# Gathering some source columns on VectorE and ScalarE: earlier address loads, 24 columns each, one-hot rows six groups ahead

## The chip, the cores and the metric

The kernel runs on one core of a Trainium2 chip. The metric is the device time of one execution in microseconds (us). Engines are named as in the profile: PE is TensorE's matrix multiplication, PEld its weight load, DVE is VectorE, ACT is ScalarE, POOL is GpSimd, SP is SyncE. PEq, DVEq and ACTq are the sequencers of those engines, which read the program in order, execute register instructions themselves and hand the others to the engine.

## The reference

One layer of a graph network on 12500 nodes with 64 features and 212500 edges with 32 features; the edges are sorted by their destination. All is float32.

```
msg_in     = concat(nodes[src], nodes[dst], edge_features)      # 212500 x 160
messages   = relu(msg_in @ mW1 + mb1) @ mW2 + mb2               # 128 hidden, 64 out
aggregated = segment_sum(messages, dst)                         # 12500 x 64
out        = layernorm(x + relu(concat(x, aggregated) @ uW1 + ub1) @ uW2 + ub2)
```

## The kernel before, in words

**Groups.** The edges are cut into G = 554 groups of 384 edges, three tiles of 128 (the last group has two). For a group the kernel needs the rows `x[src]` of its 384 edges, turned so that features lie along partitions. There are two ways to get them:

- By gather: one indirect DMA on POOL for each tile (line 165 of the profile is that call in `gather`) brings 128 rows of 64 features into `own_s`, and TensorE transposes the tile (L369) into PSUM; ScalarE copies the result into `own_st` (L380).
- By column copies: the whole transposed node table lies on the chip in `own_xc`, one column of 64 features for each node. For the first tile of some groups (the list `COPIED`, the "columned" groups) no gather is issued. Instead 128 small instructions copy one column each, from an address held in a register, straight into `own_st`: a COPY on VectorE (L539) or an ACTIVATE on ScalarE (L541). The copied groups' first tile is still transposed, but only its one-hot part is taken.

In each step COLS = 44 columns are copied, in four blocks: 12 and 8 on VectorE (`VCOLS`), 12 and 12 on ScalarE (`ACOLS`). So 128 columns, one tile, are ready every 128/44 = 2.9 steps, and 180 of the 1661 tiles need no gather; 1481 gathers are left. The addresses of a block's columns are read from a small table (`index`) into registers of the engine's own sequencer by one TENSOR_LOAD (function `registers`, L520; `fetch` then issues the copies). The copies start with step BEGIN = 18 and end ten steps before the last (`SHORT`).

**One step.** Step k, for most of the loop, gives TensorE one unbroken run of matrix multiplications over three groups: the transposes of group k (L369), the hidden layer of group k-2 (L395), and the sums of group k-4 by destination (L423, and the edge counts, L428). One signal at the end of the run releases what follows: ScalarE's copy (L380), VectorE's ReLU (L406), and VectorE's two additions of the sums into `own_agg` and of the counts into a row of `own_xc` (L437, L438). The results lie in two sets of PSUM buffers that alternate, so the run of step k starts after the ReLU, the copy and the additions of step k-2.

**The one-hot rows** (L357): VectorE compares each edge's destination with the 32 nodes of the group's window and writes three 128x32 patterns beside the gathered rows. The transposes of group k wait for them; they are written two groups ahead, in step k-2, between VectorE's two blocks of columns.

**Order.** The program's order on each engine is that in which the code issues it. In a step before the change, VectorE's order is: ReLU, TENSOR_LOAD of 12 addresses (queued in `between` and issued inside `add`, ahead of the first addition), two additions, 12 copies, one-hot rows of group k+2, TENSOR_LOAD of 8 addresses, 8 copies. ScalarE's is: copy L380 (two, for a columned group), TENSOR_LOAD of 12, 12 copies, TENSOR_LOAD of 12, 12 copies. Once in four steps VectorE's sequencer also loads the four start nodes of the next groups (`places`, L319), and once in eight VectorE turns a fresh table of node numbers into addresses (L505).

**POOL** gathers in program order, group k+16 being issued in step k. A ring of 20 buffers (`RING`) holds the gathered rows, so a gather waits at most for the transposes of the group 20 before. SP moves edge features, window rows and address tables.

**Updates.** Whenever a chunk of 512 nodes has all its edges (25 chunks, one about every 23 steps), six small stages of the node update are spread over six steps (`step_update`), each behind TensorE's run of the step: matrix products (L448 to L450, L462, L463), ReLU and square root on ScalarE (L456, L478), statistics and scaling on VectorE (L471, L472, L483, L486).

## Time and profile before

| what | value |
|---|---|
| time, median of 3 runs (lowest to highest) | 1880.31 us (1878.53 to 1881.24) |
| the profiled execution's own time | 1876.62 us |
| its span, first to last instruction | 1874.9 us |
| mean granted TensorE clock | 0.967 |
| busy share of the span: PE, DVE, ACT, POOL | 76%, 80%, 83%, 75% |
| memory traffic over the span | 53 GB/s |

The span is what the trace covers; the execution's own time is 1.7 us more. A row of the timeline gives start, duration, engine, line, operation, tiles and count, and in brackets how long the engine had sat idle before it and who ended that. A row of the waits gives the total, the number of times and the longest. A row that groups a line's instructions gives the busy time, the mean of one, and the idle time before them. TENSOR_LOAD is a sequencer's instruction and not counted as busy; it is seen when a line's instructions are asked for, with its shortest, median and longest duration.

### The profile page before, as it was taken

Reading aid. Unit: us, or ns where it says so; the run is one execution under the profiler, and the core shown is the slowest. Engines: PE = TensorE matmul, PEld = TensorE weight load, DVE = VectorE, ACT = ScalarE, POOL = GpSimd, SP = SyncE. Lnnn points to the kernel's source line nnn. Section 1 sums busy time; section 2 is a strip of 40 time slices with the busy share of each in tenths; the row PEclk is TensorE's granted clock in tenths of the full one; section 3 lists DMA queues with packets and bytes.
Section 4 is the critical chain, followed back from the end, with each engine's and each line's share of the span. In section 5 each row is a group of like instructions: output and inputs, shape, how many; then the busy total and the mean of one; then the engine's idle time right before and its main releaser. Section 6 shows DMA issues by size and latency. Waiting matters only on the chain. (4 is left out here: it accounts for less than half of the span.)

```text
span 1874.9 us, 61070 instructions
## 1 busy us (share of the span) xinstructions
PE 1429.1 (76%) x12373; PEld 1252.6 (67%) x12373; DVE 1491.0 (80%) x13140; ACT 1552.1 (83%) x13372; POOL 1399.1 (75%) x1488
## 2 busy tenths in 40 slices
PE   3898878778777778687776786776877777867777
PEld 3886667677676677576665676665656666666665
DVE  2458888888888888887887878878888788787873
ACT  3268998988998988988988889889888888898971
POOL 7777777777777777777777777777777777777773
PEclk9999999999999999999999989999999999999998
DMA  4442222222122212211221212212121212121220
GB/s 126 134 117 61 51 53 49 51 53 52 47 54 53 51 48 54 50 49 47 52 54 46 53 47 52 52 46 54 49 49 50 51 49 53 45 55 48 51 50 22
DMA packets 94294, 104.48 MB, mean 56 GB/s; under 512 B 39230, under 2 KB 61366, under 8 KB 93910
## 3 DMA queue, kind: packets, MB, share of 16 engines
q0 software_dynamic: 47392, 48.60, 11.7%
q1 hardware_dynamic: 45888, 51.46, 9.6%
q14 instruction: 280, 2.29, 0.4%
q8 instruction: 104, 1.70, 0.4%
q10 hardware_dynamic: 630, 0.43, 0.1%
HBM read 90.61 MB, written 9.62 MB: 53 GB/s over the span
## 5 line engine op out<-in xcount | busy, mean ns | idle before, releaser
L165 POOL DMA_INDIRECT own_s<-in_x,src_sb x1481 | 1398.4, 944 | 452.5 <-issue 303.3
L541 ACT ACTIVATE own_st<-own_xc 64x4 uint8 x12560 | 1268.1, 192 | 64.3 <-issue 56.0
L539 DVE COPY own_st<-own_xc 64x4 uint8 x10480 | 893.8, 190 | 20.8 <-issue 1.1
L369 PE MATMUL own_ps<-own_ident,own_s 128*96 128x128 f32 x1661 | 292.3, 287 | 396.8 <-issue 116.7
L395 PE MATMUL own_ps<-own_wm,own_st 128*128 128x128 f32 x3322 | 482.7, 284 | 0.0
L423 PE MATMUL own_ps<-own_s,own_h 128*128 128x128 f32 x3322 | 480.0, 282 | 2.6 <-DVE own_h L406 2.0
L369 PEld LDWEIGHTS own_ps<-own_ident,own_s 128*96 128x96 f32 x1661 | 171.1, 134 | 463.4 <-issue 234.9
L380 ACT ACTIVATE own_st<-own_ps 96x384 f32<-96x384 f32 (+2 forms) x734 | 294.0, 401 | 190.2 <-PE own_ps L428 149.3
L423 PEld LDWEIGHTS own_ps<-own_s,own_h 128*128 128x128 f32 x3322 | 433.4, 199 | 5.0 <-DVE own_h L406 3.8
L395 PEld LDWEIGHTS own_ps<-own_wm,own_st 128*128 128x128 f32 x3322 | 434.4, 199 | 1.8 <-issue 0.8
L406 DVE TENSOR_SCALAR own_h<-own_ps 128x384 f32<-128x384 f32 x553 | 302.0, 546 | 141.4 <-PE own_ps L428 97.3
L437 DVE TENSOR_TENSOR own_agg<-own_ps,own_agg 128x32 f32 x554 | 106.0, 191 | 147.2 <-DVE own_h L406 95.1
L428 PE MATMUL own_ps<-own_s,own_one 128*1 128x32 f32 x3322 | 188.8, 194 | 0.0
L428 PEld LDWEIGHTS own_ps<-own_s,own_one 128*1 128x1 f32 x3322 | 113.6, 83 | 69.1 <-issue 4.9
L438 DVE TENSOR_TENSOR own_xc<-own_ps,own_xc 1x32 f32 x554 | 102.0, 184 | 48.4 <-PE u_ps L450 31.7
L357 DVE TENSOR_TENSOR own_s<-iota,dlc 128x96 f32<-128x96 f32 x554 | 137.4, 248 | 0.7
L331 PE MATMUL u_ps<-w1b,own_xc 65*128 65x128 f32 x196 | 52.0, 416 | 30.9 <-DMA own_wm<-in_mW 16.3
L331 PEld LDWEIGHTS u_ps<-w1b,own_xc 65*128 65x128 f32 x196 | 47.2, 324 | 33.2 <-DMA own_wm<-in_mW 16.2
L462 PE MATMUL u_ps<-u,u 128*128 128x64 f32 (+1 forms) x196 | 63.1, 405 | 0.5 <-ACT u L456 0.5
L463 PE MATMUL u_ps<-same,own_xc 65*128 65x64 f32 (+1 forms) x196 | 62.3, 403 | 0.0
L462 PEld LDWEIGHTS u_ps<-u,u 128*128 128x128 f32 (+1 forms) x196 | 54.2, 325 | 2.4 <-ACT u L456 0.8
L463 PEld LDWEIGHTS u_ps<-same,own_xc 65*128 65x128 f32 (+1 forms) x196 | 54.9, 328 | 0.0
(60 smaller groups left out, 268.2 us busy)
## 6 DMA issues: line engine op xcount, KB each, us to landing
own_st<-in_efT SPq DMA_DIRECT2D x138, 192.0 KB
own_s<-in_x,src_sb POOLq DMA_INDIRECT x1481
own_wm<-by_dst SPq DMA_DIRECT2D x554, 16.0 KB
by_dst<-t SPq DMA_DIRECT2D x24, 256.0 KB
out<-o SPq DMA_DIRECT2D x24, 128.0 KB
own_xc<-in_xT SPq DMA_DIRECT2D x12, 179.2 KB
index<-in_src_copied SPq DMA_DIRECT2D x65, 1.4 KB
dlc_i<-in_dst_cols SPq DMA_DIRECT2D x1, 831.0 KB
```

Source lines behind the costliest of these rows:

```text
L165: nc.gpsimd.indirect_dma_start(out=s[:p, j, :D], out_offset=None, in_=x[:, :], in_offset=bass.IndirectOffsetOnAxis(ap=src_sb[:p, g * TG + ...
L357: places_by[g] = nc.vector.tensor_tensor(own.s[g % RING][:, :, D:], iota.unsqueeze(1).to_broadcast([P, TG, W]), dlc[:, g * TG : (g + 1) * ...
L369: nc.tensor.transpose(xt[:, j * P : j * P + p], s[:p, j, :], ident[:p, :p])
L380: after(nc.scalar.activation(t[r, c : c + n][:, m], xt[r, m], AF.Copy), step))
L395: nc.tensor.matmul(pre[:p, j, :], t[:, c + j * P : c + j * P + p], wm[g % NW], start=True, stop=True)
L406: relu_by[g] = [nc.vector.tensor_scalar(h, pre, 0.0, None, ALU.max)]
L423: did.append(nc.tensor.matmul(sg, h[:p, j, :], s[:p, j, D:].unsqueeze(1).to_broadcast([p, TIMES, W]), start=j == 0, stop=j == len(sizes) - 1))
L428: did.append(nc.tensor.matmul(counted, own.one[:p], s[:p, j, D:], start=j == 0, stop=j == len(sizes) - 1))
L462: nc.tensor.matmul(y[:p, k], u[:, k:q:n], u2, start=True, stop=False)
L463: nc.tensor.matmul(y[:p, k], xc[: D + 1, base + k : base + q : n], same, start=False, stop=True)
L539: by[engine] = nc.vector.tensor_copy(o, x_at)
L541: by[engine] = nc.scalar.activation(o, x_at, AF.Copy)
```

## The change

Four things are done. VectorE copies 12 and 12 columns in a step, not 12 and 8, so that COLS is 48; with that the list `COPIED` has 196 groups, and 1465 gathers are left. The first TENSOR_LOAD of VectorE and that of ScalarE are issued ahead of the step, that is ahead of the ReLU and of copy L380, and no longer behind them. The two additions follow the ReLU with nothing between. The one-hot rows are written six groups ahead (`LEAD`), not two.

VectorE's order in a step is then: TENSOR_LOAD of 12, ReLU, two additions, 12 copies, one-hot rows of group k+6, TENSOR_LOAD of 12, 12 copies. ScalarE's is: TENSOR_LOAD of 12, copy L380, 12 copies, TENSOR_LOAD of 12, 12 copies.

```diff
+LEAD = 6
-VCOLS = (12, 8)
+VCOLS = (12, 12)
 ...
             count = xc[COUNT : COUNT + 1, at]
-            if between:
-                between.pop()()
             a = after(nc.vector.tensor_tensor(agg[:, at], sg[:, 0, :], agg[:, at], ALU.add), step)
 ...
-    onehot(0)
-    onehot(1)
+    for g in range(LEAD):
+        onehot(g)
 ...
         if k < G - SHORT:
-            between.append(lambda: registers(k, 0))
+            registers(k, 0)
+            registers(k, len(VCOLS))
             step((turn, k), *([(hidden, k - 2)] if k > 1 else []),
                  *([(sums, k - 4)] if k > 3 else []))
             made, summed = max(0, k - 1), max(0, k - 3)
-            if between:
-                between.pop()()
-            fetch(0)
+            fetch(0, len(VCOLS))
 ...
         window(k + SB)
-        onehot(k + 2)
+        onehot(k + LEAD)
         if k < G - SHORT:
             for part in range(1, len(VCOLS + ACOLS)):
-                registers(k, part)
-                fetch(part)
+                if part != len(VCOLS):
+                    registers(k, part)
+                    fetch(part)
```

More of the change, by code (lines that the diff above doesn't have):

```diff
@@ L588, in ordered @@
     made = summed = 0
-    between, held = [], {}
+    held = {}
     for k in range(G):
```

## The prediction, made before the change was run

> **What bounds the kernel now.** The page comes first: its first line, the busy shares, the costliest group.

> ```profile
> span 1874.9 us, 61070 instructions
> PE 1429.1 (76%) x12373; PEld 1252.6 (67%) x12373; DVE 1491.0 (80%) x13140; ACT 1552.1 (83%) x13372; POOL 1399.1 (75%) x1488
> L165 POOL DMA_INDIRECT own_s<-in_x,src_sb x1481 | 1398.4, 944 | 452.5 <-issue 303.3
> ```

> No engine looks full, and POOL looks idlest of the four. That misleads: a gather takes 944 ns and has (452.5 / 1481 =) 306 ns of idle time ahead of it. The waits tell what that idle time is.

> ```profile
> POOL own_s L165 <- issue: 303.3, 995, 0.3
> ...
> POOL own_s L165 <- DMA own_s<-in_x,src_sb: 116.1, 381, 0.3
> ...
> DVE own_agg L437 <- DVE own_h L406: 95.1, 232, 0.9
> ...
> ACT own_st L541 <- issue: 56.0, 176, 0.7
> ```

> Whatever is named as the releaser, POOL's longest gap is 0.3 us, as long as the mean one. So POOL waits for nothing; 0.3 us is what lies between any two gathers, and POOL is full from end to end: (1398.4 + 452.5) / 1481 = 1.25 us a gather, 1851 of 1875 us. A step has 3 - 44/128 = 2.656 gathers, 3.32 us. **POOL sets the pace.** With 48 columns a step has 2.625 gathers, 3.28 us.

> Can the others follow that? Around 400 us, where POOL is still groups ahead, the timeline shows them at their own pace. VectorE:

> ```profile
> 402.43 0.54 DVE L406 TENSOR_SCALAR own_h<-own_ps 128x384 f32<-128x384 f32 x1
> 402.97 0.19 DVE L437 TENSOR_TENSOR own_agg<-own_ps,own_agg 128x32 f32 x1
> 403.19 0.18 DVE L438 TENSOR_TENSOR own_xc<-own_ps,own_xc 1x32 f32 x1
> 403.41 0.94 DVE L539 COPY own_st<-own_xc 64x4 uint8 x12
> 404.27 0.24 DVE L357 TENSOR_TENSOR own_s<-iota,dlc 128x96 f32<-128x96 f32 x1
> ...
> 405.00 0.54 DVE L406 TENSOR_SCALAR own_h<-own_ps 128x384 f32<-128x384 f32 x1
> 406.02 0.19 DVE L437 TENSOR_TENSOR own_agg<-own_ps,own_agg 128x32 f32 x1 [0.48 <-DVE own_h L406]
> 406.24 0.18 DVE L438 TENSOR_TENSOR own_xc<-own_ps,own_xc 1x32 f32 x1
> 406.46 0.97 DVE L539 COPY own_st<-own_xc 64x4 uint8 x12
> ...
> 408.08 0.54 DVE L406 TENSOR_SCALAR own_h<-own_ps 128x384 f32<-128x384 f32 x1
> ...
> 410.74 0.54 DVE L406 TENSOR_SCALAR own_h<-own_ps 128x384 f32<-128x384 f32 x1
> ```

> Copies start 0.072 us apart (403.41 to 404.27 holds twelve). From ReLU to ReLU it is 2.57, 3.08, 2.66 us. What holds VectorE up is not on the page at all: the TENSOR_LOADs of its sequencer. Asked for by line, in short stretches (the third row, of ScalarE, for comparison):

> ```profile
> L520 DVEq TENSOR_LOAD <-index x1: 593/593/593, 403.6 to 403.6; - x1
> L520 DVEq TENSOR_LOAD <-index x1: 846/846/846, 405.0 to 405.0; - x1
> L520 ACTq TENSOR_LOAD <-index x4: 772/778/786, 402.9 to 407.1; - x4
> L520 DVEq TENSOR_LOAD <-index x2: 593/720/848, 406.7 to 407.6; - x2
> L319 DVEq TENSOR_LOAD <-start_i x139: 339/344/626, 12.3 to 1841.7; - x139
> ```

> Eight addresses take 0.59 us, twelve 0.85, and meanwhile the sequencer hands its engine nothing; the engine lives on what it was handed before. Three things are read from these rows:

> - *How far the sequencer gets ahead.* The load of eight starts 0.2 us behind the first copy of a block (403.6 for 403.41, 406.7 for 406.46). The third copy is then running, and nine copies and the one-hot rows have been handed on: ten instructions, no more.
> - *How fast it hands on.* From the load of eight (406.7, ends 0.59 later) to the load of twelve (407.6) it hands on eight copies and the ReLU, in 0.3 to 0.4 us, taken as 0.37: 0.04 each, less than the 0.072 that a copy runs.
> - *What a load costs that nothing covers.* The load of 405.0 stood behind the ReLU of 405.00 and ended at 405.85; the addition came at 406.02. Of that 0.17, 0.08 is the addition's own address arithmetic; an instruction follows a load by 0.09.

> A walk along VectorE's sequencer, load of eight to load of eight, gives 0.59 + 0.37 + 0.85 + 0.17 + 0.22 + 0.22 + 0.20 = 2.62 us; the timeline has 2.66. With the start nodes' load in a step, 0.34 more, it has 3.08. The walk holds, and VectorE today has over half a microsecond to spare in POOL's 3.32.

> **The change, part by part.**

> *16 gathers fewer.* 16 x 1.25 = 20 us, if POOL still sets the pace.

> *ScalarE.* It keeps its 24 columns.

> ```profile
> 402.39 0.47 ACT L380 ACTIVATE own_st<-own_ps 96x384 f32<-96x384 f32 x1
> 402.76 2.39 ACT L541 ACTIVATE own_st<-own_xc 64x4 uint8 x24
> 405.16 0.66 ACT L380 ACTIVATE own_st<-own_ps 32x128 f32<-32x128 f32 x2
> ```

> From copy to copy 2.77 us, columns without a break. Its loads are 0.78 against 12 x 0.1 us of columns; the moved load lies beneath the last ten columns (0.95 us) of the step before. ScalarE stays near 2.8 us and gains at most the 56 us of the last waits row above, off the path.

> *VectorE, the second block: 8 to 12.* The load is 0.85 for 0.59, and four more instructions are handed on at 0.04: 0.26 + 0.16 = 0.42 us more along the walk.

> *VectorE, the first load ahead of the ReLU.* Before, this load was handled while VectorE ran the last copies and the ReLU (0.54), and only its end showed. Now the ReLU itself stands behind it, and with the ReLU the additions. What can run beneath it is the rest of the second block: twelve copies are 0.86 us of work, but they start only 0.09 behind the second load and 0.48 of them pass while they are being handed on, so about 0.45 is left against 0.85 + 0.09. **VectorE stands idle for about 0.5 us in each step** unless it would be waiting for TensorE anyway. The new walk, second load to second load:

> second load 0.85; twelve copies handed on 0.48; first load 0.85; ReLU starts 0.09; ReLU to addition 0.54 (402.43 to 402.97); addition to addition 0.22; to the first copy 0.22; to the next second load 0.20. Sum **3.45 us**. The start nodes' load (0.34 and 0.04 to hand it on, one step in four) adds 0.10: **3.55 us**, against POOL's 3.28.

> No row shows this order, so I bound it. If no load ever showed, a step is the engine's work: 0.54 + 0.44 + 24 x 0.072 + 0.24 = 2.95 us. If nothing covered them, 2.95 + 1.70 = 4.65 us. I take 3.45 because the same walk gives the present order to 0.04 us.

> [...]

> *Is TensorE ready?* If its run ended late, the first load would lie beneath that wait. It doesn't: TensorE's run that released the ReLU of 408.08 ended with

> ```profile
> 406.38 0.34 PE L428 MATMUL own_ps<-own_s,own_one 128*1 128x32 f32 x6
> ```

> at 406.72, 1.36 us earlier, and the next run needs only the additions of two steps before. With VectorE slower it waits longer. POOL, ahead at 3.28, is stopped by its ring of 20, which costs nothing.

> *The additions right behind the ReLU* end the 95 us of the waits, all from ReLU to addition; they come back as the idle time ahead of the ReLU, counted above. *One-hot rows six ahead* are the same instructions earlier; a run that waits for additions does not notice. Four more ahead of the loop are 4 x 0.24, 1 us at most. SP's transfers stay as they are.

> *Updates.* VectorE's part adds to a step that it bounds:

> ```profile
> L486 DVE TENSOR_SCALAR o<-u_ps,mv,rstd 128x64 f32<-128x64 f32 x96 | 26.4, 337 | 1.0
> ...
> L471 DVE BATCH_NORM_STATS2 stats<-u_ps 128x6 f32<-128x64 f32 x96 | 19.9, 207 | 1.1 <-PE u_ps L463 0.6
> L472 DVE BATCH_NORM_AGGREGATE mv<-stats 128x2 f32<-128x6 f32 x96 | 17.5, 182 | 3.3
> ```

> (26.4 + 19.9 + 17.5) / 24 = 2.66 us an update, 23 of them inside the loop: 61 us.

> *The sum*, with the transposes counted in three stretches:

> ```profile
> 0.00:138.00 138.00, 14.76 (x78) 12.64 (x78) 0.98 0.46 127
> 138.00:1811.00 1673.00, 270.83 (x1545) 154.10 (x1545) 0.97 0.21 51
> 1811.00:1875.00 64.00, 6.73 (x38) 4.35 (x38) 0.89 0.12 29
> ```

> Three transposes are a step: 26 steps of start, bound by first loads and left at 138 us; 515 steps with columns; a tail without columns, left at 64 us (a few less, as no gather is awaited there). 138 + 515 x 3.55 + 61 + 64 = 2091 us of span. The profiled execution took 1876.62 us, 1.7 more than its span, so 2093; the median of the runs lies 3.7 us above that execution: **2097 us, 11% slower**.

> **The rivals.**

> *POOL stays the pace (faster).* Then 16 gathers go: 1876.6 - 20 + 3.7 = 1860 us. For it: the moved loads are free wherever the engine waits for TensorE, and the two last waits rows show 95 and 56 us of such standing. It decides if a plain step of VectorE is at most 3.28 - 0.10 - 0.12 (update, 61 / 515) = 3.06 us, that is if 0.4 us more of the first load were covered. Against it: let a run of TensorE end on POOL's beat. VectorE starts its second load 1.18 us later, ends it at 2.03, has handed on the block at 2.51, ends the first load at 3.36, and the ReLU comes at 3.45, late for 3.28 with nothing else in the step. 0.11.

> *Half of the idle time is covered* (the sequencer starts its second load sooner than the rows show, or copies lie longer beneath the first): 3.30 us by 515 is 129 us less, 1968 us, counted from 1960 to 2030. 0.10.

> *A shorter queue than ten.* [...] 0.04.

> *The change does nothing of the kind* (VectorE's extra work and the 16 gathers cancel): 1880 us. 0.02.

> **How the numbers follow.** The forecast, 2097, has 0.70, with a range of its own of 2030 to 2150 (a step of 3.43 to 3.65). Something slower still without a place of its own has 0.03. 1960 to 2150 takes in forecast and half cover, 0.80. Measurement of this kernel can tell 0.2%, 4 us, from no change: faster 0.11, same 0.02, slower 0.87.

> **What would show it.** Right: from ReLU to ReLU 3.4 to 3.6 us all through the run; a gap of some 0.5 us ahead of each ReLU, with a TENSOR_LOAD of 0.85 in it; ReLU to addition always 0.54; TensorE and ScalarE waiting for VectorE; gaps of POOL well over 0.3 us. Wrong: POOL's gaps still 0.3 us at 1465 gathers, or ReLUs 3.3 us apart that start as TensorE's run ends. The sum fails if the second load starts earlier than 1.2 us behind the ReLU, or if an update costs other than 2.7 us.

## The result, and the profile after

The changed kernel takes 2073.39 us (median of 4 runs, 2069.49 to 2075.81), the kernel before beside it 1880.46: a ratio of 1.103, 95% interval 1.102 to 1.105. The forecast was 2097, the range 1960 to 2150. The profiled execution took 2073.34 us, its span 2071.5.

The page of the changed kernel, whose lines answer to the first ones shown of before (L166 is the gather, L370 the transposes, L381 ScalarE's copy, L407 the ReLU):

```profile
span 2071.5 us, 63093 instructions
PE 1459.8 (70%) x12373; PEld 1278.8 (62%) x12373; DVE 1667.8 (81%) x15212; ACT 1531.0 (74%) x13364; POOL 1384.9 (67%) x1472
...
L166 POOL DMA_INDIRECT own_s<-in_x,src_sb x1465 | 1384.1, 945 | 601.5 <-issue 394.9
...
L407 DVE TENSOR_SCALAR own_h<-own_ps 128x384 f32<-128x384 f32 x553 | 307.6, 556 | 289.8 <-PE own_ps L429 153.5
```

The 16 gathers are gone, and a gather takes what it took (945 ns). But the idle time ahead of the gathers has risen from 452.5 to 601.5 us: POOL waits now. The idle time ahead of the ReLU has doubled, from 141.4 us in the trace of before to 289.8. VectorE's share of busy time, 81% for 80%, shows nothing of this, although VectorE is now what everything waits for. The waits of the changed kernel:

```profile
POOL own_s L166 <- issue: 394.9, 1265, 5.2
...
PE own_ps L370 <- ACT own_st L381: 368.1, 268, 2.8
ACT own_st L381 <- PE own_ps L429: 328.0, 318, 9.8
POOL own_s L166 <- PE own_ps L429: 194.5, 164, 5.9
```

POOL's longest gap was 0.3 us and is 5.9: it is stopped by its ring. ScalarE's copies wait for TensorE (328 us). And TensorE, by the name in the second row, waits for ScalarE's copy. That name is wrong, and the timeline of the three engines shows how one finds out. VectorE, two steps, the first cut short, and the beginning of a third:

```profile
1213.39 0.56 DVE L407 TENSOR_SCALAR own_h<-own_ps 128x384 f32<-128x384 f32 x1 [0.29 <-PE own_ps L429]
1213.87 0.18 DVE L436 TENSOR_TENSOR own_agg<-own_ps,own_agg 128x32 f32 x1
1214.08 0.18 DVE L437 TENSOR_TENSOR own_xc<-own_ps,own_xc 1x32 f32 x1
...
1217.63 0.56 DVE L407 TENSOR_SCALAR own_h<-own_ps 128x384 f32<-128x384 f32 x1 [0.68 <-issue]
1218.10 0.18 DVE L436 TENSOR_TENSOR own_agg<-own_ps,own_agg 128x32 f32 x1
1218.32 0.18 DVE L437 TENSOR_TENSOR own_xc<-own_ps,own_xc 1x32 f32 x1
1218.53 1.01 DVE L538 COPY own_st<-own_xc 64x4 uint8 x12
1219.46 0.24 DVE L358 TENSOR_TENSOR own_s<-iota,dlc 128x96 f32<-128x96 f32 x1
1219.67 0.99 DVE L538 COPY own_st<-own_xc 64x4 uint8 x12
1220.97 0.56 DVE L407 TENSOR_SCALAR own_h<-own_ps 128x384 f32<-128x384 f32 x1 [0.32 <-issue]
```

ScalarE's copy and TensorE's runs at the same place:

```profile
1213.17 0.47 ACT L381 ACTIVATE own_st<-own_ps 96x384 f32<-96x384 f32 x1
```

```profile
1212.72 0.34 PE L429 MATMUL own_ps<-own_s,own_one 128*1 128x32 f32 x6
1214.37 0.50 PE L370 MATMUL own_ps<-own_ident,own_s 128*96 128x128 f32 x3 [1.31 <-ACT own_st L381]
...
1216.14 0.34 PE L429 MATMUL own_ps<-own_s,own_one 128*1 128x32 f32 x6
```

The copy ends at 1213.64; the run starts 0.73 us later. VectorE's second addition ends at 1214.08 + 0.18 = 1214.26, and the run starts 0.11 us behind that. Over the steps between 300 and 1800 us, three quarters of TensorE's runs start 0.10 us behind that addition; in the trace of before the least was 1.21. A run starts after the additions of two steps before, so the run of 1214.37, released by the addition of 1214.08, belongs to the third ReLU shown, that of 1220.97. It ended at 1216.48, 4.5 us before that ReLU; the run before it, which belongs to the ReLU of 1217.63, ended at 1213.06, 4.57 us before. So these ReLUs don't wait for TensorE, and the name in the bracket of the first one (its own run had ended at 1210.13) is wrong too. From 1217.63 to 1220.97 it is 3.34 us, and of the 0.32 us of idle time ahead of the ReLU of 1220.97 the sequencer's loads are the cause:

```profile
L519 DVEq TENSOR_LOAD <-index x2: 846/850/853, 1218.7 to 1220.0; - x2
```

Two loads of 0.85 us, 1.3 us from start to start; the second ends at 1220.89, and the ReLU of 1220.97 comes 0.09 us behind it.

### The profile page after: what moved, and what is told of

It is laid out like the page before. It is cut to its first block, busy times and chain, and to the rows that moved or that the text cites. A ratio compares the mean times of both kernels' runs of the same rounds, so it can differ in the third digit from the quotient of the medians.

```text
span 2071.5 us, 63093 instructions
## 1 busy us (share of the span) xinstructions
PE 1459.8 (70%) x12373; PEld 1278.8 (62%) x12373; DVE 1667.8 (81%) x15212; ACT 1531.0 (74%) x13364; POOL 1384.9 (67%) x1472
## 4 chain that ended last, share of the span: by engine, by line
PE 48%; ACT 23%; issue 13%; DVE 9%; DMA 3%; ACTq 3%; DVEq 1%; SPq 0%
PE own_ps L424 13%; PE own_ps L396 13%; ACT own_st L540 13%; ACT own_st L381 10%; PE own_ps L370 9%; DVE own_st L538 6%; PE own_ps L429 5%; ACTq L519 3%; PE u_ps L461 2%; PE u_ps L462 2%; PE u_ps L332 1%; DMA by_dst<-t 1%; PE u_ps L447 1%; PE u_ps L449 1%; PE u_ps L448 1%
## 5 line engine op out<-in xcount | busy, mean ns | idle before, releaser
L166 POOL DMA_INDIRECT own_s<-in_x,src_sb x1465 | 1384.1, 945 | 601.5 <-issue 394.9
L540 ACT ACTIVATE own_st<-own_xc 64x4 uint8 x12536 | 1245.6, 192 | 0.5
L538 DVE COPY own_st<-own_xc 64x4 uint8 x12552 | 1031.3, 184 | 35.3 <-issue 7.9
L370 PE MATMUL own_ps<-own_ident,own_s 128*96 128x128 f32 x1661 | 298.2, 291 | 537.0 <-ACT own_st L381 368.1
L381 ACT ACTIVATE own_st<-own_ps 96x384 f32<-96x384 f32 (+2 forms) x750 | 299.8, 400 | 438.4 <-PE own_ps L429 328.0
L370 PEld LDWEIGHTS own_ps<-own_ident,own_s 128*96 128x96 f32 x1661 | 173.1, 135 | 603.6 <-ACT own_st L381 387.0
L407 DVE TENSOR_SCALAR own_h<-own_ps 128x384 f32<-128x384 f32 x553 | 307.6, 556 | 289.8 <-PE own_ps L429 153.5
L424 PE MATMUL own_ps<-own_s,own_h 128*128 128x128 f32 x3322 | 493.2, 288 | 2.6 <-DVE own_h L407 2.0
L396 PE MATMUL own_ps<-own_wm,own_st 128*128 128x128 f32 x3322 | 492.5, 287 | 0.0
L424 PEld LDWEIGHTS own_ps<-own_s,own_h 128*128 128x128 f32 x3322 | 446.5, 204 | 5.0 <-DVE own_h L407 3.8
L396 PEld LDWEIGHTS own_ps<-own_wm,own_st 128*128 128x128 f32 x3322 | 444.2, 203 | 2.0 <-issue 0.8
L437 DVE TENSOR_TENSOR own_xc<-own_ps,own_xc 1x32 f32 x554 | 101.9, 184 | 20.2 <-PE u_ps L449 2.9
L436 DVE TENSOR_TENSOR own_agg<-own_ps,own_agg 128x32 f32 x554 | 100.7, 182 | 12.3 <-PE own_ps L429 10.2
```

Source lines behind the costliest of these rows:

```text
L166: nc.gpsimd.indirect_dma_start(out=s[:p, j, :D], out_offset=None, in_=x[:, :], in_offset=bass.IndirectOffsetOnAxis(ap=src_sb[:p, g * TG + ...
L370: nc.tensor.transpose(xt[:, j * P : j * P + p], s[:p, j, :], ident[:p, :p])
L381: after(nc.scalar.activation(t[r, c : c + n][:, m], xt[r, m], AF.Copy), step))
L396: nc.tensor.matmul(pre[:p, j, :], t[:, c + j * P : c + j * P + p], wm[g % NW], start=True, stop=True)
L407: relu_by[g] = [nc.vector.tensor_scalar(h, pre, 0.0, None, ALU.max)]
L424: did.append(nc.tensor.matmul(sg, h[:p, j, :], s[:p, j, D:].unsqueeze(1).to_broadcast([p, TIMES, W]), start=j == 0, stop=j == len(sizes) - 1))
```

## The experiments

**Theory A** is the prediction's: along VectorE's sequencer the first load, ahead of the ReLU, has too little work beneath it, and together with the longer second block a step costs more than POOL's. **Rivals**: B, the place of the load alone is the cost; C, 24 columns are too many for VectorE in any order; D, ScalarE's moved load or the one-hot rows six ahead have a part in it.

Only two of the twelve runs came to a chip that runs the kernel before at 1881 us. The chips of the other ten ran it at 2417 to 2452, with pauses between the instructions of ScalarE and VectorE that the trace of the kernel before, taken on a chip that ran it at 1880 us, doesn't show (the kernel before itself had a granted TensorE clock of 0.85 to 0.88 there, and of 0.96 to 0.97 on the chips at 1880 us); what makes them pause stayed open. Totals on those chips stand close together and say little; single undisturbed steps do. The pauses, in the waits of the first run below (the kernel before had 56.0 us and 176 times in this row):

```profile
ACT own_st L540 <- issue: 371.7, 645, 1.2
```

**The load back behind the ReLU, and the control, on the chip at 1881 us.** The control is the changed kernel itself. What `between` holds is issued inside `add`, ahead of the first addition, as in the kernel before.

```diff
             count = xc[COUNT : COUNT + 1, at]
+            if between:
+                between.pop()()
 ...
-            registers(k, 0)
+            between.append(lambda: registers(k, 0))
             registers(k, len(VCOLS))
```

> The changed kernel itself, as a control for the chip. The two chips of the eight runs so far ran the kernel before at 2417 and 2452 us, with pauses of 0.4 to 1.4 us between ScalarE's and VectorE's instructions that the first profile of the kernel before doesn't have. On a chip that runs the kernel before at 1880: 2073 us. On a chip that pauses: theory A has a plain step of VectorE of 3.34 us (at its fastest) where the kernel before has 2.64 and the run of loads ahead with 20 columns 2.93, so it should stand 2 to 10% above the kernel before; a control within 0.5% of it would say that totals on such a chip tell nothing of the change.

> The changed kernel with VectorE's first load back between ReLU and first addition, beside the control on the same chip. Theory A: 1855 to 1880 us where the kernel before takes 1880, and 190 to 215 us less than the control; on a chip that pauses, less than the control by 2% or more, and within 1% of the kernel before. Rival C (24 columns are too many for VectorE in any order): as slow as the control. Rival D (ScalarE's load ahead or the one-hot rows six ahead cost part of it): halfway.

The kernel before took 1881.27 us, the control 2071.37 (2073 was expected), the load put back 1966.94 (1.046 of before, 1.043 to 1.049). So the load's place alone is worth 104 us with 24 columns, over half of the loss, and rival C falls in its strong form. But theory A had 1855 to 1880, and that fell too. VectorE of this run:

```profile
1001.39 0.54 DVE L407 TENSOR_SCALAR own_h<-own_ps 128x384 f32<-128x384 f32 x1
1001.96 0.19 DVE L438 TENSOR_TENSOR own_agg<-own_ps,own_agg 128x32 f32 x1
...
1004.38 0.54 DVE L407 TENSOR_SCALAR own_h<-own_ps 128x384 f32<-128x384 f32 x1
1005.40 0.19 DVE L438 TENSOR_TENSOR own_agg<-own_ps,own_agg 128x32 f32 x1 [0.47 <-DVE own_h L407]
...
1007.85 0.54 DVE L407 TENSOR_SCALAR own_h<-own_ps 128x384 f32<-128x384 f32 x1
1008.77 0.19 DVE L438 TENSOR_TENSOR own_agg<-own_ps,own_agg 128x32 f32 x1 [0.38 <-DVE own_h L407]
```

The first step is the walk: 2.99 us for 3.00. The next is 3.47. Over 297 plain steps between 300 and 1800 us the mean is 3.27: the fastest tenth are at 2.99 or less, but from ReLU to addition it is 0.71 us on average for 0.55 when the load is covered. Part of that is the start nodes' load. In this order its delay shows behind the next ReLU, in the step after the one that holds it: the 3.47 us shown are such a step, and the mean of the 99 plain steps that follow a start nodes' load is 3.45, with 0.90 from ReLU to addition. The other 198 have a mean of 3.19, still 0.19 over the walk, so the walk was a best case here. What makes that 0.19 is not shown. (The 0.38 us ahead of the last addition shown is no part of it: no load stands there, and only 3 of the 438 steps have such a gap.) A reading that fits is that VectorE's engine has 2.9 us of work in a step and its sequencer 3.0, so that when either is held up for a moment the other has no reserve. With updates and start nodes the step is 3.42 us (515 steps from 140 to 1902 us), still above POOL's 3.28. That ScalarE isn't the cause shows in the waits of this run:

```profile
ACT own_st L381 <- PE own_ps L429: 231.7, 245, 9.4
```

ScalarE's copy starts 0.04 us behind TensorE's run in the median, while the ReLU starts 3.2 us behind it. That speaks against the half of rival D that lies on ScalarE. The one-hot rows six ahead were not tried apart, but the traces speak against that half too: the rows take VectorE 246 ns in this run and in the changed kernel, 248 before, and the only waits for them are TensorE's in the kernel before:

```profile
PE own_ps L369 <- DVE own_s L357: 32.2, 37, 1.9
```

No wait of the two later traces is put down to them.

**Loads ahead, 20 columns** (three runs, each on a chip with pauses).

```diff
-VCOLS = (12, 12)
+VCOLS = (12, 8)
```

> The changed kernel with VectorE's columns put back to 12 and 8 (44 columns a step, 1481 gathers); loads ahead of the step, additions right behind the ReLU and one-hot rows six ahead are kept. Theory A (it takes both: the load that stands uncovered ahead of the ReLU and the longer second load, along VectorE's sequencer): load of 8 0.59, eight copies handed on 0.30, load of 12 0.85, ReLU 0.09 later, then 0.47, 0.22, 0.21 and 0.20 as measured in the changed kernel: 2.93 us, with start nodes (0.10) and updates (0.13) 3.16, under POOL's 3.32. So POOL keeps the pace: 1870 to 1885 us, POOL's gaps 0.3 us. Rival B (the place of the first load alone is the cost): 0.4 us by 520 steps more, 2050 to 2100 us.

> The changed kernel with VectorE's columns at 12 and 8 (1481 gathers) once more, since the chip of the first four runs ran the kernel before at 2452 us. Theory A: a plain step of VectorE 2.93 us (the shortest steps of the first run were 2.92 to 2.96), 3.16 with start nodes and updates, POOL's 3.32 ends last: 1870 to 1885 us on a chip that runs the kernel before at 1880. Rival B (the place of the first load alone is the cost): 2050 to 2100 us.

> The changed kernel with VectorE's columns at 12 and 8 (1481 gathers), all else of the change kept, hoped for on a chip that runs the kernel before at 1880 us. With the load behind the ReLU and 24 columns the kernel took 1967: 104 us under the control's 2071, but 86 over the kernel before, where theory A had it at POOL's pace. What costs the 86? Theory A2 (VectorE's 24 columns: engine 2.9 and sequencer 3.0 us a step lie so close that every stall of the one starves the other, 3.27 on average for a plain step): here engine 2.6 and walk 2.93 lie apart, 3.16 to 3.25 with start nodes and updates, POOL's 3.32 ends last: 1870 to 1900 us. Rival D (ScalarE's load ahead or the one-hot rows six ahead cost the 86): at least 1960 us here. Rival B (the load's place alone costs 104 or more, whatever the columns): 1980 us or more.

2463.61 us beside 2452.00 (1.002 to 1.006), 2432.31 beside 2417.36 (1.005 to 1.010), 2463.74 beside 2448.62 (1.003 to 1.008). In the totals the load's place costs 0.5%, not the 5% or more of rival B; but the pauses could hide part of it, so against B this is strong and not final. What can be read is a plain step that no pause has touched (a tenth of the 243 plain steps of the second run are at 2.96 us or less; with the pauses the mean is 3.99). VectorE in the second of these runs:

```profile
1148.40 0.56 DVE L407 TENSOR_SCALAR own_h<-own_ps 128x384 f32<-128x384 f32 x1 [0.70 <-issue]
...
1150.33 0.65 DVE L538 COPY own_st<-own_xc 64x4 uint8 x8
1151.38 0.56 DVE L407 TENSOR_SCALAR own_h<-own_ps 128x384 f32<-128x384 f32 x1 [0.40 <-issue]
...
1154.34 0.56 DVE L407 TENSOR_SCALAR own_h<-own_ps 128x384 f32<-128x384 f32 x1 [0.31 <-issue]
```

2.98 and 2.96 us, for 2.93 by the walk. So the load ahead costs VectorE 0.3 us a step by itself (2.66 before). By these steps POOL's 3.32 would have room for it, and it is the four columns more, 0.4 us, that use up that room; on a chip at 1881 us no run of this order was had, so that stays argued.

**The columns alone, and the load behind the additions** (chips with pauses). The first is the kernel before with nothing else changed, the second the changed kernel with its first load moved.

```diff
-VCOLS = (12, 8)
+VCOLS = (12, 12)
```

> The kernel before with VectorE's columns at 12 and 12 and nothing else changed (48 columns, 1465 gathers; first loads behind ReLU and ScalarE's copy, one-hot rows two ahead). Theory A: load 0.85, thirteen handed on 0.49, load 0.85, then 0.17, 0.22, 0.22, 0.20: 3.00 us, with start nodes and updates 3.23, just under POOL's 3.28: 1855 to 1890 us. Rival C (24 columns are more than VectorE can do in any order: its engine work and two loads of 12): 2000 us or more, like the changed kernel.

```diff
-            registers(k, 0)
             registers(k, len(VCOLS))
...
+            registers(k, 0)
             fetch(0, len(VCOLS))
```

> The changed kernel with VectorE's first load moved once more: behind the two additions, ahead of the first block's copies (so the additions still follow the ReLU at once; 24 columns each). Theory A: now the sequencer itself is the limit: load 0.85, twelve copies, ReLU and additions handed on 0.75, load 0.85, twelve copies and one-hot rows handed on 0.55: 3.0 us, 3.25 with start nodes and updates, about POOL's 3.28: 1855 to 1890 us. Rival (the additions' new place, not the load's, made TensorE late): as slow as the changed kernel, 2073 us.

The columns alone: 2464.73 beside 2452.00 (1.003 to 1.009). The load behind the additions: 2428.45 beside 2417.36 (1.004 to 1.011). The load behind the ReLU, on the same two chips:

> The changed kernel with one thing put back: VectorE's first load stands again between the ReLU and the first addition. ScalarE's load stays ahead, 24 columns each and one-hot rows six ahead stay. Theory A: VectorE's walk as in the run of the columns alone, 3.23 us a step, POOL's 3.28 ends last: 1855 to 1880 us. Rival C: 2000 us or more. Rival D (ScalarE's load ahead, or the one-hot rows six ahead, cost part of the 193 us): between, 1900 to 2000 us.

> The changed kernel with VectorE's first load back between ReLU and first addition, once more for the same reason. Theory A: 3.00 us a plain step of VectorE, 3.23 in all, POOL's 3.28 ends last: 1855 to 1880 us where the kernel before takes 1880. Rival C (24 columns are too many for VectorE in any order): 2000 us or more. Rival D (ScalarE's load ahead or the one-hot rows six ahead cost part of the 193 us): 1900 to 2000 us.

2461.28 beside 2452.00 (1.001 to 1.008) and 2439.47 beside 2417.36 (1.005 to 1.011). None of the three orders with 48 columns is faster than the kernel before, though each saves 16 gathers; more can't be read from totals under such pauses, and all of these are inconclusive between A and C. The changed kernel itself was not run on these chips, so the rival on the additions' place stays open. For rival D there is a comparison on one chip: the load behind the ReLU differs from the columns alone by ScalarE's moved load and the one-hot rows six ahead, and takes 2461.28 for 2464.73, no difference that these totals could tell.

**Four more columns on ScalarE, not VectorE** (chips with pauses). The first of three runs had 14 and 14, the two others 16 and 12.

```diff
-VCOLS = (12, 12)
-ACOLS = (12, 12)
+VCOLS = (12, 8)
+ACOLS = (14, 14)
...
-            registers(k, 0)
+            between.append(lambda: registers(k, 0))
```

> The changed kernel with VectorE's load back between ReLU and addition and VectorE's columns at 12 and 8, ScalarE's at 14 and 14: again 48 columns and 1465 gathers, but the four more are ScalarE's. Theory A: VectorE 2.62 + 0.23 = 2.85 us a step; ScalarE 0.37 + 28 x 0.095 = 3.03, 0.19 more for a step with two copies, 3.14 with updates; both under POOL's 3.28, with more room than any other order of 48 columns: 1855 to 1865 us. Rival (ScalarE becomes the pace, its loads of 14 uncovered): 3.4 us or more, 1930 us or more.

> As the run of 28 columns on ScalarE, but in blocks of 16 and 12, not 14 and 14 (VectorE 12 and 8, its first load between ReLU and addition; 48 columns, 1465 gathers). Theory E on the loads of 14, which took 1.22 and 3.02 us where 12 take 0.78: a load goes fast by fours of addresses that start at a multiple of 16 bytes, and address by address (0.22 us each) elsewhere. Then 16 and 12, all of whose blocks start at such multiples, take about 1.04 and 0.78 us, ScalarE's step is 3.14 us, and POOL's 3.28 ends last: 1855 to 1865 us. Rival (a load of more than 12 addresses is slow as such): the load of 16 takes 1.4 to 3.5 us, ScalarE sets the pace, 1950 us or more.

> 48 columns in which ScalarE takes 16 and 12 and VectorE 12 and 8, VectorE's first load behind the ReLU, one-hot rows six ahead, ScalarE's first load ahead of the step; hoped for on the same quiet chip. Theory A2: VectorE is as in the kernel before (2.64 a plain step), ScalarE has 0.37 + 28 x 0.095 = 3.03 and 0.19 more with two copies, without the stalls that VectorE shows, 3.15 to 3.2 with updates; POOL's 3.28 ends last: 1855 to 1875 us, below both kernels. Rival D: 1960 us or more. Rival E (ScalarE so near to POOL's pace is the next VectorE): 1900 to 1960 us.

With 14 and 14: 3202.94 beside 2452.00, 1.306 (1.300 to 1.312). Theory A fails; the rival, that ScalarE becomes the pace with its loads uncovered, holds, and far above its 1930 us. ScalarE's idle time ahead of its columns is 1052.8 us in this run (56.0 in the kernel before). Two of its loads side by side in this run, and two with 16 and 12:

```profile
L521 ACTq TENSOR_LOAD <-index x2: 1222/2114/3005, 1598.5 to 1602.0; - x2
```

```profile
L521 ACTq TENSOR_LOAD <-index x2: 774/898/1022, 1199.6 to 1200.8; - x2
```

1.22 and 3.0 us for fourteen addresses each; 1.02 for sixteen and 0.77 for twelve. That is what theory E, on the loads of fourteen, had. With 16 and 12 the kernel takes 2465.04 beside 2417.36 (1.019 to 1.025) and 2499.02 beside 2448.62 (1.018 to 1.025): 2% slower than before, where 1% faster was expected of a quiet chip. Whether it would win without pauses wasn't found out. No run beat the kernel before.

## Why the prediction was right

*POOL set the pace before, and no longer does.* POOL's longest gap rose from 0.3 to 5.9 us.

*VectorE's walk*, term by term, as means of the 283 plain steps between 300 and 1800 us of the trace after, with the forecast behind: second load 0.85 (0.85); twelve copies handed on 0.48 (0.48); first load 0.85 (0.85); ReLU behind it 0.10 (0.09); ReLU to addition 0.47 (0.54); addition to addition 0.22 (0.22); to the first copy 0.22 (0.22); to the next second load 0.21 (0.20). Sum 3.40, for 3.45. **The one term of the walk that was mis-sized is the ReLU to addition.** 0.54 was read from a step in which the addition's own address arithmetic and the load stood between; right behind the ReLU it takes 0.47.

*The start nodes' load* was forecast at 0.10 for each step. A step that holds it alone takes 3.79, which gives that 0.10. But in every second of these steps VectorE also turns a fresh table of node numbers into addresses (L504 here); those take 3.95, and the 0.02 a step that this adds is in no term of the forecast. *Updates* were forecast at 2.66 us each. A step that holds a part of one takes 4.84, 1.33 more than the mean of all others (3.51, start nodes' loads included), and an update has two such steps: 2.65 us. Together (2009.6 - 139.4) / 515 = 3.63 us a step, for 3.55 + 61/515 = 3.67. *The start* took 139.4 us for 138, *the tail* 61.9 for 64. The 20 us between 2091 and the span of 2071.5 are nearly all those 0.04 us by 515: 0.07 less from ReLU to addition, and small terms the other way.

*How far the sequencer gets ahead.* The second load starts 0.19 to 0.20 us behind the first copy in three quarters of the plain steps after, so nine copies and the one-hot rows were again handed on: ten, in an order that no row had shown. No run shows a shorter queue, to which the prediction gave 0.04.

*TensorE was ready* before nearly every ReLU, as forecast (6 of 413 between 300 and 1800 us start within 0.06 us of the end of their run): the median ReLU of the trace after starts 3.8 us behind the end of its run, and in nine of ten plain steps it starts 0.09 behind the load.

*The rival on the other side*, that POOL stays the pace, was priced too kindly. It was to decide at 3.06 us for a plain step. The run with the load behind the ReLU has 2.99 at its fastest tenth, and still lost 86 us: the decision hangs on the mean (3.19 even without the steps that follow a start nodes' load), and not on the undisturbed step. In the changed kernel the mean (3.40) and the undisturbed step (3.33 to 3.34) lie close, and that is why the walk served so well there. A reading that fits, but that no run tests, is that its engine idles in each step and takes up the stalls.

## What to carry to other kernels

VectorE had two clocks to keep here: its own work, 2.95 us a step by the prediction's estimate, and its sequencer's, 3.40 in a plain step of the changed kernel. The two loads of 0.85 us in that step appear in no busy share (VectorE's was 80% before and 81% after), so walk the sequencer's program once round a step, with each load's duration, what was handed on beforehand and what still runs beneath it. Before moving a load ahead of an instruction, see whether that instruction waits. In the changed kernel only 6 of 413 ReLUs started within 0.06 us of the end of TensorE's run, and the load, out of the cover of the work it stood behind, cost 104 us (2071.37 for 1966.94); a gain from such a move is shown by no run. And where engine and sequencer come as near to each other and to the pace as in the run with the load behind the ReLU (2.9, 3.0 and 3.28 us), count on the mean step (3.27 there), not on the clean one (2.99).

## What the runs showed of the hardware that was not expected

The load behind a ReLU that waited was held with it. In the trace of before, where VectorE had stood idle for over 0.1 us ahead of a ReLU (90 steps), the load behind it started 0.014 us after the ReLU's start in the median, and 0.024 at most. That moving the load ahead can win this wait is the author's estimate; no run shows it.

A name in the waits was wrong by a whole engine: in the trace after, 368 us of TensorE's idle time stand under ScalarE's copy, which in the step looked at had ended 0.73 us before, while VectorE's addition had ended 0.11 us before.
